# Router logits of fourteen batches computed on GpSimd instead of TensorE, and the choice of experts one batch later, in a fused decoder layer

## The chip, the core and the metric

The kernel runs on one core of a Trainium2 chip. The metric is device time in microseconds for one execution, as the median of several runs. The engines are TensorE (PE; its weight loads are shown as PEld), VectorE (DVE), ScalarE (ACT), GpSimd (POOL) and SyncE (SP, which issues most of the DMAs). Each engine works through its own instructions in a fixed order, and waits for other engines by semaphores.

## The reference

The computation is one decoder layer on x of 16 batches x 256 rows x 256 columns, in float32. It has three stages, each followed by a layer normalization of input plus result:

1. a recurrent block: an input projection to 512 channels, a causal convolution over 4 positions, silu, a projection to 2 x 16 state terms, a scan along the 256 rows, and an output projection;
2. cross attention with 8 heads of 128: queries from x (256 rows), keys and values from 77 context rows and the 256 rows of x (333 in all), softmax, output projection;
3. a mixture of 8 experts. The router is the part that the change touches:

```python
dot = jnp.einsum('bsh,eh->bse', x, expert_embeddings)   # 256 columns -> 8 logits a row
vals, idx = jax.lax.top_k(dot.reshape(n, E), 2)
weights = softmax(where(chosen, dot, -inf))
ones = weights > 0
cap_ones = where(cumsum(ones, axis=0) <= 512, ones, 0)  # each expert takes its first 512 rows
# the chosen rows go through relu(rows @ W1.T) @ W2.T, times the weight, and are added up
```

So for each row of each batch eight dot products of length 256 are needed, then the two largest, then a running count over all rows in order.

## The kernel before

**Tiling.** Rows lie on the 128 partitions; a batch is two tiles of 128 rows. Batches are worked on one after the other, and inside a batch the 8 heads, so the main loop has 128 turns. In turn i TensorE does the key and query products of head i (L512, L517), then the extra steps that are planned for this head, then the output of head i-2 (L564), the scores s of head i (L527), and the transposes pa and pb of head i-1's softmax (L550). VectorE takes the row maximum nm of s (L529), copies the transposed pa to SBUF as ptt (L552), takes the reciprocal rs of the sums (L535) and scales p to pn (L538). ScalarE does exp and most of the copies out of PSUM. GpSimd does small work: the -1/2 powers of the normalizations (r..., L134, called by `rsqrt`), adding the output bias to x (xb, L596), sums of hs for the recurrent block (L305), sums of kvt (tsum, L460 to L463), the output rows o (L624), and the indirect DMAs.

**Extra steps.** A table gives each (batch b, head h) the steps that ride along: `project(b-1)` (the pw products and the second normalization) at heads 2 and 3, `turn_tokens(b-1)` at head 5, `score_experts(b-1)` and `choose(b-1)` at head 6, `dispatch(b-1)` at head 7, `settle(b-1)` (output rows o) at head 7. The steps for the next batch ride there too: in an odd batch `rec_add` and `rec_out` (first normalization of the next two batches) at heads 1 and 3, `prep_norm`, `prep_keys` and `prep_sums` (zl, kvt, tsum), and `prep_values` (pv). The convolutions of the recurrent block (`rec_in`, four chunks for each pair of batches, cv at L297 and L299, hs at L303) ride in batches 0, 1, 2, 4, 5, 6, 8, 9 and 10; in batches 2, 6 and 10 they are at heads 3, 4, 5 and 7, in the others at single heads. The scheduler may move an instruction ahead of that place on its own engine.

**The router before.** `turn_tokens` transposes the normalized rows xs on TensorE (px, four 128x128 products, L649) and VectorE copies them to SBUF (L650). `score_experts` multiplies them by the experts' vectors emb_s (pl, eight products of 8 columns, L658), and VectorE copies the 2 x 8 logits of a row (L666). `choose` finds the two largest with some twenty VectorE instructions of 128x16 or less (L683 to L716). `dispatch` counts with two small products on TensorE (pc, L725, L726), works out the places on VectorE (L728 to L757), and issues four indirect DMAs on GpSimd (L760) that write the rows to their experts. The last two batches (14 and 15) are handled near the end in the same way, at earlier heads.

**Normalization factors.** `again` (L156 to L160, and the power at L134) makes the second factor rlz on GpSimd, which `prep_norm` multiplies into the rows: zl (L425, VectorE), which TensorE then transposes for the keys.

After the main loop the eight experts are worked through (L956 to L1064), some 120 us.

Of the kernel before, what the change touches and what calls it, by code (L numbers as in the profile page):

```python
# [10 lines left out]
F32 = mybir.dt.float32  # L11
I32 = mybir.dt.int32
AF = mybir.ActivationFunctionType
ALU = mybir.AluOpType
AX = mybir.AxisListType
# [3 lines left out]
P = 128  # L19
B, S, D = 16, 256, 256  # L20
# [3 lines left out]
J = S + M  # L24
DI = 512
NST = 16
KC = 4
# [5 lines left out]
GT = S // P  # L33
# [5 lines left out]
def decoder_layer(  # L39
# [20 lines left out]
    bkv,  # L60
    wo,
    bo,
    embT,
    w1T,
    w2T,
# [60 lines left out]
    def apart(group, dma):  # L126
# [2 lines left out]
            tc.declare_no_dep(dma.ins, other.ins, reason="disjoint rows")  # L129
        groups.setdefault(group, []).append(dma)  # L130

    def rsqrt(v, n, rows, name):
        r = small.tile([P, n], F32, tag="r", name=f"r{name}")
        G.tensor_tensor(r[:rows], v[:rows], nhalf[:rows, 0:n], ALU.pow)  # L134
        return r

    def layernorm(dst, src, n, rows, name):
# [42 lines left out]
    gl = wpool.tile([P, DC], F32, tag="gl", name="gl")  # L180
    bl = wpool.tile([P, DC], F32, tag="bl", name="bl")
    emb_s = wpool.tile([P, DC, E], F32, tag="emb", name="emb_s")
    wsum = wpool.tile([P, 4, 512], F32, tag="wsum", name="wsum")

    kvc = wpool.tile([P, DC, B * M], F32, tag="kvc", name="kvc")
# [72 lines left out]
    def load_rest():  # L258
        nc.sync.dma_start(wo_s, wo.rearrange("(h p) f -> p h f", p=P))
        nc.sync.dma_start(bo_s, bo.broadcast_to([P, D]))  # L260
        nc.sync.dma_start(emb_s, embT.rearrange("(c p) e -> p c e", p=P))
    zero = wpool.tile([P, DX], F32, tag="zero", name="zero")
    G.memset(zero, 0.0)
# [18 lines left out]
    def rec_in(pr, c):  # L282

        if c == 0:
            hss[pr] = aw.tile([P, NI, PT], F32, tag="hs", bufs=2, name=f"hs{pr}")
            if pr > 0:
                sums[pr] = aw.tile([P, PT], F32, tag="sums", bufs=2, name=f"sums{pr}")
        ph = bank(f"ph{pr}_{c}")
        for k in range(DC):
            T.matmul(ph, lhsT=inw[:, k, c * P : (c + 1) * P], rhs=xTs[pr][:, k, :], start=(k == 0), stop=(k == DC - 1))  # L290
        hp = a2.tile([P, PB, KC - 1 + S], F32, tag="hp", name=f"hp{pr}_{c}")
        G.memset(hp[:, :, 0 : KC - 1], 0.0)
        A.activation(
            hp[:, :, KC - 1 :], ph.rearrange("p (b s) -> p b s", b=PB), AF.Identity, bias=inb[:, c : c + 1]
        )
        cv = a2.tile([P, PB, S], F32, tag="cv", name=f"cv{pr}_{c}")
        V.tensor_scalar(cv, hp[:, :, 0:S], cw[:, c, 0:1], cb[:, c : c + 1], ALU.mult, ALU.add)  # L297
        for k in range(1, KC):
            V.scalar_tensor_tensor(cv, hp[:, :, k : k + S], cw[:, c, k : k + 1], cv, ALU.mult, ALU.add)  # L299
        z = cv.rearrange("p b s -> p (b s)")  # L300
        th = a2.tile([P, PT], F32, tag="th", name=f"th{pr}_{c}")
        A.activation(th, z, AF.Tanh)
        V.scalar_tensor_tensor(hss[pr][:, c, :], th, 1.0, z, ALU.add, ALU.mult)  # L303
        if c > 0 and pr > 0:
            G.tensor_tensor(sums[pr], hss[pr][:, 0, :] if c == 1 else sums[pr], hss[pr][:, c, :], ALU.add)  # L305

# [110 lines left out]

    stages = {}

    def prep_norm(b):  # L420

        r2 = again(*stats.pop(b), f"z{b}")
        zl = b2.tile([P, 2, D], F32, tag="zl", name=f"zl{b}")
        for i in range(2):
            V.tensor_scalar(zl[:, i, :], xs[b][:, i, 0:D], r2[:, i : i + 1], None, ALU.mult)  # L425
        zs[b] = zl
# [95 lines left out]
    def head_softmax(b, h):  # L522

        kt, qt = kts.pop((b, h)), qts.pop((b, h))
        s = ps.tile([P, 2, 512], F32, tag="s", bufs=1, name=f"s{b}_{h}")
        for ic in range(2):
            T.matmul(s[:, ic, 0:J], lhsT=qt[:, ic * P : (ic + 1) * P], rhs=kt, start=True, stop=True)  # L527
        nm = small.tile([P, 2], F32, tag="nm", name=f"nm{b}_{h}")
        V.tensor_reduce(nm, s[:, :, 0:J], AX.X, ALU.max, negate=True)  # L529
        p = b2.tile([P, 2, J], F32, tag="p", name=f"p{b}_{h}")  # L530
        sm = small.tile([P, 2], F32, tag="sm", name=f"sm{b}_{h}")
        for ic in range(2):
            A.activation(p[:, ic, :], s[:, ic, 0:J], AF.Exp, bias=nm[:, ic : ic + 1], accum_out=sm[:, ic : ic + 1])  # L533
        rs = small.tile([P, 2], F32, tag="rs", name=f"rs{b}_{h}")
        V.reciprocal(rs, sm)  # L535
        pn = b2.tile([P, 2, J], F32, tag="pn", name=f"pn{b}_{h}")
        for ic in range(2):
            V.tensor_scalar(pn[:, ic, :], p[:, ic, :], rs[:, ic : ic + 1], None, ALU.mult)  # L538
        pns[b, h] = pn

    def head_turn(b, h):

# [33 lines left out]
    def project(b, i):  # L576

        ot = outs_t[b]
        if i == 0 or b == B - 1:
            pws[b] = bank(f"pw{b}_{i}")  # L580
        for h in range(H):
            T.matmul(  # L582
                pws[b][:, i * D : (i + 1) * D],
                lhsT=ot[:, h, i * P : (i + 1) * P],
                rhs=wo_s[:, h, :],
                start=(h == 0),
                stop=(h == H - 1),
            )
        if b == B - 1:
            norm_half(b, i)  # L590
            return
        if i == 0:
            return
        xb = b1.tile([P, 2, D], F32, tag="xb", name=f"xb{b}")
        for j in range(2):
            G.tensor_tensor(xb[:, j, :], xs[b][:, j, 0:D], bo_s, ALU.add)  # L596
        y = b2.tile([P, 2, D], F32, tag="yb", name=f"yb{b}")
        V.tensor_tensor(y.rearrange("p i d -> p (i d)"), pws.pop(b), xb.rearrange("p i d -> p (i d)"), ALU.add)  # L598
        norms[b] = layernorm(xs[b], y, 2, P, f"b{b}")

    def norm_half(b, i):

# [16 lines left out]
    def settle(b):  # L619

        r2 = again(*norms.pop(b), f"o{b}")
        o = b2.tile([P, 2, D], F32, tag="yb", name=f"o{b}")
        for j in range(2):
            G.tensor_scalar(o[:, j, :], xs[b][:, j, 0:D], r2[:, j : j + 1], 1.0, ALU.mult, ALU.mult)  # L624
        nc.sync.dma_start(out_f[b * S : (b + 1) * S, :].rearrange("(i p) d -> p i d", p=P), o)
# [26 lines left out]
    def score_experts(b):  # L652

        x2 = x2s.pop(b)
        pl = bank(f"pl{b}")
        for i in range(2):
            for k in range(DC):
                T.matmul(  # L658
                    pl[:, i * E : (i + 1) * E],
                    lhsT=x2[:, k, i * P : (i + 1) * P],  # L660
                    rhs=emb_s[:, k, :],
                    start=(k == 0),
                    stop=(k == DC - 1),
                )
        lgs[b] = small.tile([P, GT, E], F32, tag="lg", bufs=2, name=f"lg{b}")
        V.tensor_copy(lgs[b].rearrange("p t e -> p (t e)"), pl[:, 0 : GT * E])  # L666

    def t3(tag, b):
        return small.tile([P, GT, E], F32, tag=tag, bufs=2, name=f"{tag}_{b}")
# [104 lines left out]
    def at(b, h, f, *args):  # L774
        steps[b, h].append((f, args))

    def behind(b, h, f, *args):

        late_steps[b, h].append((f, args))
# [4 lines left out]
    for b in range(B):  # L784
        nb = b + 1
        new_pair = nb % PB == 0 and nb < B
        if b > 0:
            early = 2 * int(b == B - 1)
            at(b, 2, project, b - 1, 0)
            at(b, 3 - early // 2, project, b - 1, 1)  # L790
            at(b, 5 - early, turn_tokens, b - 1)
            at(b, 6 - early, score_experts, b - 1)
            at(b, 6 - early, choose, b - 1)
            at(b, 7 - early, dispatch, b - 1)
            at(b, 7, settle, b - 1)
        if new_pair:
            if nb == PB:
                at(b, 0, rec_state, nb, nb + 1)
            elif nb % 4 == 0:
                at(b, 0, rec_state, nb, nb + 3)  # L800
            at(b, 1, rec_add, nb)
            at(b, 1, rec_out, nb)
            at(b, 2, prep_norm, nb)
            at(b, 3, rec_out, nb + 1)
            at(b, 3, prep_keys, nb)
            at(b, 3, prep_sums, nb)
            for n, h in enumerate((4, 6, 7)):
                at(b, h, prep_values, nb, n, False)
                behind(b, h, prep_values, nb, n, True)
        elif nb < B:  # L810
            at(b, 0, prep_norm, nb)
            at(b, 0, prep_keys, nb)
            at(b, 0, prep_sums, nb)
            for n, h in enumerate((1, 4, 6)):
                at(b, h, prep_values, nb, n, False)
                behind(b, h, prep_values, nb, n, True)
# [22 lines left out]
    context(3)  # L839
    rec_add(0)  # L840
    rec_out(0)
    prep_norm(0)
    prep_keys(0)
    context(4)
# [231 lines left out]
    for i in range(len(heads) + 2):  # L1076
# [12 lines left out]
            head_softmax(*heads[i])  # L1089
        if 1 <= i <= len(heads):  # L1090
            turned = head_turn(*heads[i - 1])
        if i < len(heads):
            for f, args in late_steps[heads[i]]:
                f(*args)
# [84 lines left out]
```

## Time and profile before

| what | value |
|---|---|
| median of 3 runs | 1200.22 us (1199.39 to 1200.71) |
| the profiled execution's own time | 1201.09 us |
| its span, first to last instruction | 1199.3 us |
| mean granted TensorE clock | 0.991 |
| GpSimd busy | 312.3 us (26%), 560 instructions |
| VectorE busy | 748.6 us (62%) |
| DMA queue of SP | 50.13 MB |

A group line of the profile has the line in the code, the engine, the operation, output <- inputs, partitions x elements and the count; then busy time in us (overlaps counted once), the mean ns of one instruction, and the idle time of the engine just before, with what ended it. A timeline line has the start in us from the span's start, the length in us, the engine, the line and the instruction, "x2" where two in a row are merged, and in brackets idle time before it. A tile line has minimum, median and maximum in ns. A stretch line has, after its bounds and length, the busy time (and the count) of PE, PEld, DVE, ACT and POOL, the granted clock, the DMA share and GB/s.

### The profile page before, as it was taken

What the parts mean: (1) busy time and instruction counts of PE and PEld (TensorE: products, weight loads), DVE (VectorE), ACT (ScalarE), POOL (GpSimd) and SP (SyncE); (2) the same over time, 40 slices, a digit from 0 to 9 for tenths busy, and PEclk for the clock granted to TensorE, in tenths of its full rate; (3) what the DMA queues carried; (4) which work ended last, traced back from release to release, by engine and by line L of the source; (5) the groups of instructions that cost most, each with busy time, mean ns of one, the idle gap of its engine ahead of it and who ended that gap; (6) DMA issues with size and microseconds to landing.
All of it is one profiled execution on the core that took longest, in us unless ns stands there. A gap on an engine that the chain in (4) does not pass through costs nothing. (4 is left out here: it accounts for less than half of the span.)

```text
span 1199.3 us, 15750 instructions
## 1 busy us (share of the span) xinstructions
PE 1152.6 (96%) x5134; PEld 827.8 (69%) x5134; DVE 748.6 (62%) x2226; ACT 485.4 (40%) x1273; POOL 312.3 (26%) x560
## 2 busy tenths in 40 slices
PE   6789999999999999999999999999999999999996
PEld 2337676767777767767777777677777778876664
DVE  5535768596646765874658576756465645666665
ACT  2125434444344434443435343534343433423331
POOL 2200132222221332222213222232122211225554
PEclk8899999999999999999999999999999999999999
DMA  6760001001000110010000000010001000125762
GB/s 207 226 188 11 19 20 37 28 10 56 18 29 9 35 36 23 9 46 18 15 10 23 29 21 9 4 29 4 20 14 45 14 9 3 30 92 171 182 182 85
DMA packets 45402, 60.37 MB, mean 50 GB/s; under 512 B 7813, under 2 KB 35438, under 8 KB 45320
## 3 DMA queue, kind: packets, MB, share of 16 engines
q1 hardware_dynamic: 38552, 50.13, 13.6%
q0 software_dynamic: 6048, 9.22, 3.1%
q8 instruction: 41, 0.67, 0.2%
q14 instruction: 41, 0.34, 0.1%
q10 hardware_dynamic: 720, 0.01, 0.0%
HBM read 36.07 MB, written 30.78 MB: 56 GB/s over the span
## 5 line engine op out<-in xcount | busy, mean ns | idle before, releaser
L564 PE MATMUL po<-ptt,v 128*128 128x256 f32 (+1 forms) x768 | 190.0, 382 | 6.3 <-DVE ptt L552 6.3
L564 PEld LDWEIGHTS po<-ptt,v 128*128 128x128 f32 (+1 forms) x768 | 142.7, 190 | 58.7 <-issue 25.7
L529 DVE TENSOR_REDUCE nm<-s 128x2 f32<-128x666 f32 x128 | 108.3, 846 | 117.1 <-PE s L527 117.1
L512 PE MATMUL pk<-kvt,wkv_s 128*128 128x333 f32 x512 | 164.9, 444 | 0.0
L527 PE MATMUL s<-kt,qt 128*128 128x333 f32 x512 | 164.3, 442 | 0.0
L572 ACT ACTIVATE ot<-po,bkv_s 128x256 f32<-128x256 f32 x128 | 60.8, 475 | 218.9 <-PE po L564 218.7
L533 ACT ACTIVATE p<-s,nm 128x333 f32<-128x333 f32 x256 | 135.4, 535 | 33.7 <-DVE nm L529 32.5
L517 PE MATMUL pq<-kvt,wq_s 128*128 128x256 f32 x512 | 131.2, 378 | 0.0
L512 PEld LDWEIGHTS pk<-kvt,wkv_s 128*128 128x128 f32 x512 | 91.1, 191 | 45.0 <-issue 22.0
L527 PEld LDWEIGHTS s<-kt,qt 128*128 128x128 f32 x512 | 96.4, 188 | 31.3 <-ACT qt L519 0.5
L517 PEld LDWEIGHTS pq<-kvt,wq_s 128*128 128x128 f32 x512 | 96.7, 189 | 30.2
L582 PE MATMUL pw<-wo_s,ot 128*128 128x256 f32 x512 | 115.8, 379 | 0.0
L553 ACT COPY ptt<-pb 77x256 f32<-77x256 f32 x128 | 47.1, 368 | 168.2 <-PE pb L550 168.2
L582 PEld LDWEIGHTS pw<-wo_s,ot 128*128 128x128 f32 x512 | 97.0, 190 | 13.2
L538 DVE TENSOR_SCALAR pn<-p,rs 128x333 f32<-128x333 f32 x256 | 97.8, 416 | 3.8
L760 POOL DMA_INDIRECT xg<-xs,sidx x64 | 66.4, 1038 | 88.7 <-DVE sidx L757 68.0
L550 PEld LDWEIGHTS pa<-ident,pn 128*128 128x128 f32 x512 | 63.6, 141 | 34.8 <-DVE pn L538 6.8
L552 DVE COPY ptt<-pa 128x512 f32<-128x512 f32 x128 | 87.1, 680 | 0.6 <-PE pa L550 0.6
L596 POOL TENSOR_TENSOR xb<-xs,bo_s 128x256 f32<-128x256 f32 x30 | 19.9, 683 | 244.1 <-DVE yb L598 244.1
L550 PE MATMUL pa<-ident,pn 128*128 128x128 f32 x512 | 78.3, 274 | 2.6 <-DVE pn L538 2.6
L514 ACT ACTIVATE kt<-pk,bkv_s 128x333 f32<-128x333 f32 x128 | 69.0, 539 | 19.9 <-PE pk L512 19.6
L299 DVE SCALAR_TENSOR_TENSOR cv<-hp,cw,cv 128x512 f32<-128x512 f32 x96 | 71.8, 751 | 1.9
(231 smaller groups left out, 1670.0 us busy)
## 6 DMA issues: line engine op xcount, KB each, us to landing
v<-vc SPq DMA_DIRECT2D x16, 308.0 KB
vc<-vc SPq DMA_DIRECT2D x9, 512.0 KB
xg<-zero SPq DMA_DIRECT2D x34, 131.0 KB
xe<-xg SPq DMA_DIRECT2D x8, 524.0 KB
xT<-in_xT SPq DMA_DIRECT2D x8, 512.0 KB
xt<-in_x_in SPq DMA_DIRECT2D x16, 256.0 KB
out<-o SPq DMA_DIRECT2D x16, 256.0 KB
w<-in_w1T SPq DMA_DIRECT2D x8, 512.0 KB
```

Source lines behind the costliest of these rows:

```text
L299: V.scalar_tensor_tensor(cv, hp[:, :, k : k + S], cw[:, c, k : k + 1], cv, ALU.mult, ALU.add)
L512: T.matmul(pk[:, 0:J], lhsT=wkv_s[:, k, f], rhs=kvt[:, k, :], start=(k == 0), stop=(k == DC - 1))
L514: A.activation(kt, pk[:, 0:J], AF.Identity, bias=bkv_s[:, h : h + 1])
L517: T.matmul(pq[:, 0:S], lhsT=wq_s[:, k, f], rhs=kvt[:, k, 0:S], start=(k == 0), stop=(k == DC - 1))
L527: T.matmul(s[:, ic, 0:J], lhsT=qt[:, ic * P : (ic + 1) * P], rhs=kt, start=True, stop=True)
L529: V.tensor_reduce(nm, s[:, :, 0:J], AX.X, ALU.max, negate=True)
L533: A.activation(p[:, ic, :], s[:, ic, 0:J], AF.Exp, bias=nm[:, ic : ic + 1], accum_out=sm[:, ic : ic + 1])
L538: V.tensor_scalar(pn[:, ic, :], p[:, ic, :], rs[:, ic : ic + 1], None, ALU.mult)
L550: T.transpose(dst[0:jn, c0 : c0 + P], pn[:, ic, j0 : j0 + jn], ident)
L552: turned = V.tensor_copy(ptt[:, 0:2, :], pt01.rearrange("p (j i) -> p j i", j=2))
L564: T.matmul(po[:, 0:S], lhsT=vs[b][0:jn, jc, h * DH : (h + 1) * DH], rhs=ptt[0:jn, jc, :], start=(jc == 0), stop=(jc == 2),)
L582: T.matmul(pws[b][:, i * D : (i + 1) * D], lhsT=ot[:, h, i * P : (i + 1) * P], rhs=wo_s[:, h, :], start=(h == 0), stop=(h == H - 1),)
```

## The change

For batches 0 to 13 the transposes, the logit products and their copies are gone. In their place `score` runs on GpSimd, in four parts for a batch (two row tiles x two groups of four experts). A part multiplies the row tile, repeated for four experts, by the experts' vectors, which lie on all partitions in the new tile emb_b; then it adds halves onto each other until 32 columns are left. `score_end` lets VectorE add up these 32 columns. The parts are at heads 4 to 7 of batch b for the rows of batch b-1; `score_end` and `choose` come at head 0 of batch b+1, behind the copy ptt, and `dispatch` at head 2 of batch b+1. Batches 14 and 15 keep TensorE's way.

The parts are issued after the factor rlz of a later batch (`factor_ends`), and this factor is now its own step `prep_factors`, ahead of `prep_norm`. SBUF for emb_b (8 KB a partition), the products (4 KB) and the folded parts is made by smaller changes: the tanh is written over the convolution's input hp, the softmax is scaled in place (p with three buffers, no pn), the sum y is written over xb, and zl and o have one buffer instead of two. A DMA of 1 MB brings emb_b to all partitions, after the other weights.

```diff
+    emb_b = wpool.tile([P, E, D], F32, tag="emb_b", name="emb_b")
...
+        nc.sync.dma_start(emb_b.rearrange("p e d -> p (e d)"), emb.broadcast_to([P, E * D]))
...
-        th = a2.tile([P, PT], F32, tag="th", name=f"th{pr}_{c}")
-        A.activation(th, z, AF.Tanh)
+        th = hp[:, :, KC - 1 :]
+        A.activation(th, cv, AF.Tanh)
...
+    def prep_factors(b):
+        factors[b] = again(*stats.pop(b), f"z{b}")
+        factor_ends[b] = powers[-1]
     def prep_norm(b):
-        r2 = again(*stats.pop(b), f"z{b}")
-        zl = b2.tile([P, 2, D], F32, tag="zl", name=f"zl{b}")
+        r2 = factors.pop(b)
+        zl = b1.tile([P, 2, D], F32, tag="zl", name=f"zl{b}")
...
-        p = b2.tile([P, 2, J], F32, tag="p", name=f"p{b}_{h}")
+        p = b2.tile([P, 2, J], F32, tag="p", bufs=3, name=f"p{b}_{h}")
...
-        pn = b2.tile([P, 2, J], F32, tag="pn", name=f"pn{b}_{h}")
         for ic in range(2):
-            V.tensor_scalar(pn[:, ic, :], p[:, ic, :], rs[:, ic : ic + 1], None, ALU.mult)
+            V.tensor_scalar(p[:, ic, :], p[:, ic, :], rs[:, ic : ic + 1], None, ALU.mult)
...
-        y = b2.tile([P, 2, D], F32, tag="yb", name=f"yb{b}")
-        V.tensor_tensor(y.rearrange("p i d -> p (i d)"), pws.pop(b), xb.rearrange("p i d -> p (i d)"), ALU.add)
+        flat = xb.rearrange("p i d -> p (i d)")
+        V.tensor_tensor(flat, pws.pop(b), flat, ALU.add)
...
-        o = b2.tile([P, 2, D], F32, tag="yb", name=f"o{b}")
+        o = b1.tile([P, 2, D], F32, tag="yb", name=f"o{b}")
...
+    EG = 4
+    W = 32
+    def score(b, i, g):
+        after = factor_ends.get(b + 3 if b % 2 == 0 else b + 2)
+        if after is not None:
+            with tc.issue_after(after.ins):
+                score_part(b, i, g)
+        else:
+            score_part(b, i, g)
+    def score_part(b, i, g):
+        if i == 0 and g == 0:
+            parts[b] = b1.tile([P, GT, E, W], F32, tag="x2", name=f"part{b}")
+        x = xs[b][:, i, 0:D].unsqueeze(1).broadcast_to([P, EG, D])
+        e = slice(g * EG, (g + 1) * EG)
+        m = b1.tile([P, EG, D], F32, tag="prod", name=f"prod{b}_{i}_{g}")
+        G.tensor_tensor(m, x, emb_b[:, e, :], ALU.mult)
+        n = D // 2
+        while n > W:
+            G.tensor_tensor(m[:, :, 0:n], m[:, :, 0:n], m[:, :, n : 2 * n], ALU.add)
+            n //= 2
+        G.tensor_tensor(parts[b][:, i, e, :], m[:, :, 0:n], m[:, :, n : 2 * n], ALU.add)
+    def score_end(b):
+        lgs[b] = small.tile([P, GT, E], F32, tag="lg", bufs=2, name=f"lg{b}")
+        V.tensor_reduce(lgs[b], parts.pop(b), AX.X, ALU.add)
...
-            at(b, 5 - early, turn_tokens, b - 1)
-            at(b, 6 - early, score_experts, b - 1)
-            at(b, 6 - early, choose, b - 1)
-            at(b, 7 - early, dispatch, b - 1)
+            if b == B - 1:
+                at(b, 3, turn_tokens, b - 1)
+                at(b, 4, score_experts, b - 1)
+                at(b, 4, choose, b - 1)
+                at(b, 5, dispatch, b - 1)
+            else:
+                for n in range(4):
+                    at(b, 4 + n, score, b - 1, n // 2, n % 2)
+                settled(b + 1, 0, score_end, b - 1)
+                settled(b + 1, 0, choose, b - 1)
+                at(b + 1, 2, dispatch, b - 1)
...
+        if 1 <= i < len(heads):
+            with tc.issue_after(turned.ins):
+                for f, args in turn_steps[heads[i]]:
+                    f(*args)
```

More of the change, by code (lines that the diff above doesn't have):

```diff
@@ L62, in decoder_layer @@
     bo,
+    emb,
     embT,
@@ L130, in apart @@
         groups.setdefault(group, []).append(dma)
+    powers = []
     def rsqrt(v, n, rows, name):
         r = small.tile([P, n], F32, tag="r", name=f"r{name}")
-        G.tensor_tensor(r[:rows], v[:rows], nhalf[:rows, 0:n], ALU.pow)
+        powers.append(G.tensor_tensor(r[:rows], v[:rows], nhalf[:rows, 0:n], ALU.pow))
         return r
@@ L299, in rec_in @@
             V.scalar_tensor_tensor(cv, hp[:, :, k : k + S], cw[:, c, k : k + 1], cv, ALU.mult, ALU.add)
-        z = cv.rearrange("p b s -> p (b s)")
-        th = a2.tile([P, PT], F32, tag="th", name=f"th{pr}_{c}")
-        A.activation(th, z, AF.Tanh)
-        V.scalar_tensor_tensor(hss[pr][:, c, :], th, 1.0, z, ALU.add, ALU.mult)
+        th = hp[:, :, KC - 1 :]
+        A.activation(th, cv, AF.Tanh)
+        V.scalar_tensor_tensor(hss[pr][:, c, :].rearrange("p (b s) -> p b s", b=PB), th, 1.0, cv, ALU.add, ALU.mult)
         if c > 0 and pr > 0:
@@ L418, in decoder_layer @@
     stages = {}
+    factors, factor_ends = {}, {}
+    def prep_factors(b):
+        factors[b] = again(*stats.pop(b), f"z{b}")
+        factor_ends[b] = powers[-1]
     def prep_norm(b):
-        r2 = again(*stats.pop(b), f"z{b}")
-        zl = b2.tile([P, 2, D], F32, tag="zl", name=f"zl{b}")
+        r2 = factors.pop(b)
+        zl = b1.tile([P, 2, D], F32, tag="zl", name=f"zl{b}")
         for i in range(2):
@@ L535, in head_softmax @@
         V.reciprocal(rs, sm)
-        pn = b2.tile([P, 2, J], F32, tag="pn", name=f"pn{b}_{h}")
         for ic in range(2):
-            V.tensor_scalar(pn[:, ic, :], p[:, ic, :], rs[:, ic : ic + 1], None, ALU.mult)
-        pns[b, h] = pn
+            V.tensor_scalar(p[:, ic, :], p[:, ic, :], rs[:, ic : ic + 1], None, ALU.mult)
+        pns[b, h] = p
     def head_turn(b, h):
@@ L596, in project @@
             G.tensor_tensor(xb[:, j, :], xs[b][:, j, 0:D], bo_s, ALU.add)
-        y = b2.tile([P, 2, D], F32, tag="yb", name=f"yb{b}")
-        V.tensor_tensor(y.rearrange("p i d -> p (i d)"), pws.pop(b), xb.rearrange("p i d -> p (i d)"), ALU.add)
-        norms[b] = layernorm(xs[b], y, 2, P, f"b{b}")
+        flat = xb.rearrange("p i d -> p (i d)")
+        V.tensor_tensor(flat, pws.pop(b), flat, ALU.add)
+        norms[b] = layernorm(xs[b], xb, 2, P, f"b{b}")
     def norm_half(b, i):
@@ L666, in score_experts @@
         V.tensor_copy(lgs[b].rearrange("p t e -> p (t e)"), pl[:, 0 : GT * E])
+    EG = 4
+    W = 32
+    parts = {}
+    def score(b, i, g):
[20 more added lines that the diff above has]
+        V.tensor_reduce(lgs[b], parts.pop(b), AX.X, ALU.add)
     def t3(tag, b):
@@ L775, in at, with settled @@
         steps[b, h].append((f, args))
+    turn_steps = {(b, h): [] for b in range(B) for h in range(H)}
+    def settled(b, h, f, *args):
+        turn_steps[b, h].append((f, args))
     def behind(b, h, f, *args):
@@ L802, in decoder_layer @@
             at(b, 1, rec_out, nb)
+            at(b, 2, prep_factors, nb)
             at(b, 2, prep_norm, nb)
             at(b, 3, rec_out, nb + 1)
+            at(b, 3, prep_factors, nb + 1)
             at(b, 3, prep_keys, nb)
@@ L810, in decoder_layer @@
         elif nb < B:
+            if b == 0:
+                at(b, 0, prep_factors, nb)
             at(b, 0, prep_norm, nb)
@@ L841, in decoder_layer @@
     rec_out(0)
+    prep_factors(0)
     prep_norm(0)
@@ L1163 @@
         "bo": a[xa + "bo"].reshape(1, -1),
+        "emb": a[ff + "expert_embeddings"].reshape(1, E * D),
         "embT": a[ff + "expert_embeddings"].T,
```

## The prediction

> **What bounds the kernel now.** I read the page first. The busy rows give TensorE 96%, and the 40 slices show it at 9 from the fourth to the last but one:
>
> ```profile
> PE 1152.6 (96%) x5134; PEld 827.8 (69%) x5134; DVE 748.6 (62%) x2226; ACT 485.4 (40%) x1273; POOL 312.3 (26%) x560
> ```
>
> From 100 to 1,060 us TensorE has hardly a gap, so a matmul that goes is time that goes, unless a new gap opens. The groups by line give the matmuls that go (duration modelled, idle before them 0.0):
>
> ```profile
> L658 PE MATMUL pl<-emb_s,x 128*128 128x8 f32 x120 | 14.3, 245 | 0.0
> L649 PE MATMUL px<-ident,xs 128*128 128x128 f32 x60 | 9.0, 272 | 0.0
> ```
>
> The timeline of a batch shows the one place where TensorE waits regularly: head 3 of an odd batch, here batch 7 (start, length, engine):
>
> ```profile
> 558.11 1.54 PE L564 MATMUL po<-ptt,v 128*128 128x256 f32 x6 [0.85 <-DVE ptt L552]
> 559.48 1.28 PE L527 MATMUL s<-kt,qt 128*128 128x333 f32 x4
> 561.29 0.85 PE L550 MATMUL pa<-ident,pn 128*128 128x128 f32 x4 [0.53 <-DVE pn L538]
> ```
>
> ```profile
> 560.25 0.35 DVE L425 TENSOR_SCALAR zl<-xs,rlz 128x256 f32<-128x256 f32 x1 [2.29 <-POOL rlz L134]
> 560.52 0.16 DVE L535 RECIPROCAL rs<-sm 128x2 f32<-128x2 f32 x1
> 560.60 0.33 DVE L425 TENSOR_SCALAR zl<-xs,rlz 128x256 f32<-128x256 f32 x1
> 560.85 0.69 DVE L538 TENSOR_SCALAR pn<-p,rs 128x333 f32<-128x333 f32 x2
> ```
>
> VectorE sits behind GpSimd's factor rlz, and the transposes pa behind VectorE: no slack there. In most other heads pn is done 2.2 to 4 us before its transposes start (pn of 500.61 ends at 502.31, its pa starts at 504.69).
>
> What VectorE pays when GpSimd streams is in the tile view (min/median/max) and in the timelines of batch 6:
>
> ```profile
> L538 DVE TENSOR_SCALAR pn<-p,rs x256: 379/390/1404, 96.1 to 1051.7; 128x333 f32<-128x333 f32 x128
> ```
>
> ```profile
> 500.61 1.70 DVE L538 TENSOR_SCALAR pn<-p,rs 128x333 f32<-128x333 f32 x2
> ```
>
> ```profile
> 500.78 1.34 POOL L305 TENSOR_TENSOR sums<-hs 128x512 f32<-128x512 f32 x1 [1.83 <-DVE hs L303]
> ```
>
> A pn pair takes 0.69 us. Here it took 1.70: the GpSimd add issued during the first pn, went before the second and held it to its end. The reverse shows in the same batches: conv steps cv (two SBUF inputs) and GpSimd's output rows o hold each other (at 242.5 us one cv took 848 ns instead of 750, one o 892 instead of 482). The row maximum nm keeps 0.85 us with or without GpSimd beside it.
>
> **The change part by part.**
>
> *Removed from TensorE.* Per batch four transposes, 4 x 9.0/60 = 0.60 us, and eight logit products, 8 x 14.3/120 = 0.95. Fourteen batches: 14 x 1.55 = **-21.7 us**. The copies x (0.69) and lg (0.17) leave VectorE; a reduction of 128x512 arrives (about 0.7, from nm's 846 ns for 666 columns). Nothing.
>
> *Added to GpSimd.* Four parts per batch, each a product of 1024 columns and sums of 512, 256 and 128:
>
> ```profile
> L596 POOL TENSOR_TENSOR xb<-xs,bo_s 128x256 f32<-128x256 f32 x30 | 19.9, 683 | 244.1 <-DVE yb L598 244.1
> L305 POOL TENSOR_TENSOR sums<-sums,hs 128x512 f32<-128x512 f32 x14 | 18.2, 1297 | 24.8 <-DVE hs L303 24.8
> ```
>
> From 256 to 512 columns the step is 0.61 us, so 1024 take 1.30 + 2 x 0.61 = 2.53, and 128 take 0.46 (tsum). A part: 2.53 + 1.30 + 0.68 + 0.46 = 4.97 us; a batch 19.9; fourteen 278. GpSimd would be busy 590 us of 1,199: there is room, and the time goes by what its stream holds up.
>
> *Price of a meeting.* The held pair lost 1.01 us to an add of 1.34, so a meeting costs the GpSimd instruction less 0.33: 2.20, 0.97, 0.35 and 0.13, mean 0.91, 14.6 us per batch if every one of the 16 is met.
>
> (a) Head 3 of odd batches. In the new order the first product is the very next GpSimd instruction after rlz, so it meets zl or the reciprocal's successors. pa has no slack: 2.2 us in each of 7 odd batches, **+15.4** (bounds: 0 if zl and pn slip ahead, 7 x 2.53 = 17.7).
>
> (b) Batches 2, 6 and 10 have conv chunks in heads 3, 4 and 5, just where the parts run. VectorE is nearly full there:
>
> ```profile
> 490.80:505.40 14.60, 14.60 (x62) 9.96 (x61) 13.78 (x25) 7.73 (x19) 1.97 (x4) 1.00 0.05 18
> ```
>
> (TensorE 14.60, VectorE 13.78, GpSimd 1.97 of 14.60 us.) Each of these heads has 7 instructions that can meet: one cv scaling, three cv steps, hs, two pn; 21 against 16 parts' instructions and 4 of o and xb (together 1.0 us). What runs beside nm, ptt, rs and the v addition (0.85 + 0.68 + 0.17 + 0.68 = 2.4 of 6.4 us, 37%) costs nothing: (14.6 + 1.0) x 0.63 = 9.8, less 2.4 of slack: 7.4 us a batch, **+22** (bounds: 0, and 3 x 15.6 = 47).
>
> (c) Single chunks fall among the parts in head 5 of batches 1, 4, 5, 8 and 9: 7 x 0.91 x 0.63 = 4.0, less 2.4: 1.6 each, **+8** (0 to 32).
>
> (d) Other heads: two pn, 1.8 us, below the slack of some 2.8: 0 (the worst pair, product then 512 add, 3.2).
>
> The row comes first, but the Trainium skill speaks to the same thing: "SBUF — State Buffer", section "Who interferes with whom", says that GpSimd and VectorE share a port pair, that an instruction in a 2-port mode takes it for its whole length and the other side blocks, that two SBUF inputs on VectorE contend with GpSimd's reads, and that a reduction never does. The held pn and the unchanged nm agree. Taken literally a meeting costs the whole instruction, not 0.33 less; the sum below would then be about +46 instead of +24, an estimate from that page. It speaks against the change.
>
> *Moved.* Choice goes from head 6 to head 0 of the next batch: about 21 small VectorE instructions of 0.17 us, 3.5 us. In an odd head 0 VectorE has 1.9 us idle of 7.2, so with the reduction nm of head 1 comes 2.3 late; behind it wait exp and pn of head 1, whose slack is 4.1: 0, and up to 7 x 2.3 = 16 if that cover were gone. If GpSimd is late, the reduction stands at the front of VectorE with rs, pn and the next nm behind it. Dispatch moves to head 2: its four DMA issues (about 1.3 us apart, 5.1 us) now stand in GpSimd's queue before rb, the factor of the second normalization, which is ready only at 552.8 in batch 7 when they would run from 543.7 to 548.8: 0 (late by all of it: 14 x 5). Its two small products are moved ahead of pw on TensorE, their input is a head old: 0.
>
> *The rest.* The tanh written over hp, the softmax scaled in place with three buffers, y in xb, single zl and o: each buffer's last reader is at least a head older than the next writer (zl: read at 549.9, written at 560.3): 0. The broadcast load of 1 MB enters SP's queue after the weights, ahead of vc, xT and v; six clears move behind them: 0, at most 5.5 us at the 190 GB/s of the page's first slices.
>
> **Sum** for the profiled execution (1,201.09 us; span 1,199.3): -21.7 + 15.4 + 22 + 8 = +23.7, so 1,224.8. The median lies 0.9 lower: **1,224 us, slower**.
>
> **Rivals.**
> - *The holds are absorbed* (faster). VectorE has 38% idle, loses the copy x, and head 6 loses its choice; if zl and pn slip ahead in (a) and (b), (c) stay within the slack, the time is 1,200 - 21.7 = 1,179, with half of (a) 1,186. It decides at 21.7 us of stalls: 1.55 per batch. For it: TensorE's slack of 2 to 4 us almost everywhere. Against: (a) has none, and 13.78 of 14.60.
> - *GpSimd late.* In plain odd batches parts start at 560.2 and need 19.9, plus o, xb and 16 waits of up to 0.4: to 587 or later; tsum (1.9 us) stands behind and pv needs it at 590.9. If strided or broadcast operands make a part 2.5 us longer, 10 us a batch, 5 to 6 of it stall TensorE in some 6 batches: +33, about 1,257.
> - *A draw.* (a) in full and half of (c) and nothing else: within 2.4 us of before.
>
> **Chances.** Holds cost more than the matmuls (forecast, 1,203 to 1,250): 0.55. GpSimd late as well: 0.12. Absorbed: 0.28. Draw: 0.05. So slower by over 0.2% (about what a measurement of this kernel can tell from no change) 0.67, within 0.05, faster 0.28. The bounds of (a) to (c) reach from 1,179 to 1,275; leaving out the lowest of the faster case and the top of the late one gives 1,184 to 1,258; the forecast's own range is 1,203 to 1,250.
>
> **What would show it.** pn's and cv's maxima: pn to about 2.6 us, cv to 3, dozens of instances; nm unchanged at 0.85. TensorE's idle time before pa in odd head 3 from 0.5 to 2.7 us; gaps before pa in heads 3 to 5 of batches 2, 6 and 10; GpSimd near 590 us with products of 2.5 us. px and pl down to two batches. Wrong if pn waits but pa does not, if the products come in pieces that let VectorE through, or if GpSimd's instructions give way.

## The result, and the profile after

The changed kernel takes 1235.37 us (median of four runs, 1232.99 to 1236.41) against 1199.81 us before: ratio 1.0294, 95% interval 1.0275 to 1.0313. It is slower by some 35 us, inside the predicted range and on the predicted side, 11 us above the predicted time. Its profiled execution has a span of 1231.2 us (before: 1199.3) and a mean granted clock of 0.983 (before: 0.991).

The busy rows of the page after:

```profile
PE 1148.1 (93%) x4966; PEld 816.9 (66%) x4966; DVE 844.6 (69%) x2212; ACT 485.3 (39%) x1273; POOL 587.7 (48%) x784
```

The 168 matmuls are gone (14 x 12), yet TensorE is busy only 4.5 us less, and VectorE is busy 96 us more with 14 instructions fewer. GpSimd's 588 us are what was forecast. The groups of the page show its products (busy, mean ns of one) and the row maximum:

```profile
L699 POOL TENSOR_TENSOR prod<-xs,emb_b 128x1024 f32<-128x1024 f32 x56 | 124.0, 2215 | 2.7
...
L541 DVE TENSOR_REDUCE nm<-s 128x2 f32<-128x666 f32 x128 | 108.2, 845 | 104.2 <-PE s L539 104.2
```

The products take 2.2 us (forecast 2.5), and nm does not notice them (846 ns before, 845 after). VectorE instructions that work from SBUF to SBUF do. The tile views (minimum/median/maximum ns) of p, cv and zl:

```profile
L549 DVE TENSOR_SCALAR p<-p,rs x256: 373/395/2461, 93.4 to 1084.5; 128x333 f32<-128x333 f32 x128
```

```profile
L304 DVE SCALAR_TENSOR_TENSOR cv<-hp,cw,cv x96: 734/752/2725, 13.9 to 803.1; 128x512 f32<-128x512 f32 x96
```

```profile
L437 DVE TENSOR_SCALAR zl<-xs,rlz x32: 324/350/2433, 48.6 to 956.2; 128x256 f32<-128x256 f32 x32
```

The medians are as before and the maxima are the median plus one GpSimd product. The 48 cv steps with no GpSimd arithmetic beside them average 746 ns, the 48 with some 1,418.

**Head 3 of batch 7**, the place of step (a). Timelines of VectorE, GpSimd and TensorE (start, length):

```profile
580.90 2.43 DVE L437 TENSOR_SCALAR zl<-xs,rlz 128x256 f32<-128x256 f32 x1 [1.13 <-POOL rlz L137]
583.26 0.15 DVE L547 RECIPROCAL rs<-sm 128x2 f32<-128x2 f32 x1
583.33 0.33 DVE L437 TENSOR_SCALAR zl<-xs,rlz 128x256 f32<-128x256 f32 x1
583.58 0.68 DVE L549 TENSOR_SCALAR p<-p,rs 128x333 f32<-128x333 f32 x2
```

```profile
580.17 0.70 POOL L137 TENSOR_TENSOR rlz<-u3z,nhalf 128x2 f32<-128x2 f32 x1
580.84 2.34 POOL L699 TENSOR_TENSOR prod<-xs,emb_b 128x1024 f32<-128x1024 f32 x1
```

```profile
584.02 0.85 PE L561 MATMUL pa<-ident,p 128*128 128x128 f32 x4 [1.44 <-DVE p L549]
```

The product starts 0.06 us before zl, zl lasts until it ends (2.43 us instead of 0.35), p and the transposes pa follow late.

**Batch 6**, the place of step (b), VectorE, GpSimd and TensorE:

```profile
517.97 2.25 DVE L304 SCALAR_TENSOR_TENSOR cv<-hp,cw,cv 128x512 f32<-128x512 f32 x1
520.14 0.68 DVE L563 COPY ptt<-pa 128x512 f32<-128x512 f32 x1
```

```profile
517.67 2.00 POOL L699 TENSOR_TENSOR prod<-xs,emb_b 128x1024 f32<-128x1024 f32 x1
```

```profile
520.96 2.90 PE L575 MATMUL po<-ptt,v 128*128 128x256 f32 x6 [3.82 <-ACT hp L307]
```

A cv step is held behind a product; ptt, which is not held itself (680 ns in the mean before and after), stands behind it in VectorE's queue and ends at 520.82; po, which reads ptt, starts 0.14 us later, after 3.8 us of idle time. The profile names ScalarE's hp as the releaser, the tanh of the same held cv, because it ended last (520.94); po reads ptt, not hp. The list of TensorE's waits (total us, times, longest) has this pair 13 times, where the list of before has none:

```profile
PE po L575 <- ACT hp L307: 25.7, 13, 3.8
PE pa L561 <- DVE p L549: 9.6, 8, 1.4
```

po now takes 2.90 us for 6 matmuls instead of 1.53: the windows behind that gap show the granted clock (third figure from the end):

```profile
505.00:519.00 14.00, 11.11 (x40) 6.44 (x38) 13.89 (x14) 4.92 (x13) 13.59 (x13) 1.00 0.06 20
519.00:521.00 2.00, 0.04 (x1) 0.07 (x1) 2.00 (x4) 0.92 (x4) 1.92 (x2) 0.90 0.00 0
521.00:526.00 5.00, 5.00 (x11) 3.48 (x12) 4.96 (x6) 1.78 (x4) 4.73 (x6) 0.50 0.00 0
```

VectorE is full (13.89 of 14.00), GpSimd too, TensorE waits; and then it runs at half clock until 527.4.

**Head 0 of batches 5 and 9.** One more wait of the same list is new, and no GpSimd part runs beside it:

```profile
PE po L575 <- DVE oh L732: 3.7, 2, 1.9
```

In batches 5 and 9 the moved choice shares head 0 with a convolution chunk and the first normalization. Its small instructions stand between them in VectorE's queue, ptt comes late behind all of them (at 421.2 us in batch 5), and po waits 1.85 us in each of the two batches.

### The profile page after: what moved, and what is told of

The parts are those of the page before. It is cut to its first block, busy times and chain, and to the rows that moved or that the text cites. A ratio compares the mean times of both kernels' runs of the same rounds, so it can differ in the third digit from the quotient of the medians.

```text
span 1231.2 us, 15427 instructions
## 1 busy us (share of the span) xinstructions
PE 1148.1 (93%) x4966; PEld 816.9 (66%) x4966; DVE 844.6 (69%) x2212; ACT 485.3 (39%) x1273; POOL 587.7 (48%) x784
## 5 line engine op out<-in xcount | busy, mean ns | idle before, releaser
L575 PE MATMUL po<-ptt,v 128*128 128x256 f32 (+1 forms) x768 | 197.0, 392 | 39.1 <-ACT hp L307 25.7
L575 PEld LDWEIGHTS po<-ptt,v 128*128 128x128 f32 (+1 forms) x768 | 145.2, 194 | 98.2 <-ACT hp L307 36.1
L539 PE MATMUL s<-kt,qt 128*128 128x333 f32 x512 | 169.6, 453 | 0.0
L549 DVE TENSOR_SCALAR p<-p,rs 128x333 f32<-128x333 f32 x256 | 136.1, 567 | 3.3
L699 POOL TENSOR_TENSOR prod<-xs,emb_b 128x1024 f32<-128x1024 f32 x56 | 124.0, 2215 | 2.7
L702 POOL TENSOR_TENSOR prod<-prod 128x512 f32<-128x512 f32 x112 | 119.9, 1070 | 6.8
L539 PEld LDWEIGHTS s<-kt,qt 128*128 128x128 f32 x512 | 99.4, 194 | 32.8 <-issue 2.4
L304 DVE SCALAR_TENSOR_TENSOR cv<-hp,cw,cv 128x512 f32<-128x512 f32 x96 | 103.7, 1083 | 1.9
L561 PEld LDWEIGHTS pa<-ident,p 128*128 128x128 f32 x512 | 64.6, 143 | 43.6 <-DVE p L549 15.1
L561 PE MATMUL pa<-ident,p 128*128 128x128 f32 x512 | 80.1, 278 | 9.6 <-DVE p L549 9.6
```

Source lines behind the costliest of these rows:

```text
L549: V.tensor_scalar(p[:, ic, :], p[:, ic, :], rs[:, ic : ic + 1], None, ALU.mult)
L561: T.transpose(dst[0:jn, c0 : c0 + P], pn[:, ic, j0 : j0 + jn], ident)
L575: T.matmul(po[:, 0:S], lhsT=vs[b][0:jn, jc, h * DH : (h + 1) * DH], rhs=ptt[0:jn, jc, :], start=(jc == 0), stop=(jc == 2),)
L699: G.tensor_tensor(m, x, emb_b[:, e, :], ALU.mult)
L702: G.tensor_tensor(m[:, :, 0:n], m[:, :, 0:n], m[:, :, n : 2 * n], ALU.add)
```

## The experiments

Ratios are to runs of the kernel before on the same chip. The theory: GpSimd's arithmetic holds VectorE's SBUF instructions, and time is lost where one of these has no slack (zl in odd head 3) or many lie in a full queue (conv chunks). The rivals: GpSimd is late; the other edits (choice, buffers, load) cost it; VectorE is too full wherever the work lies.

**1. Logits on TensorE, all other edits kept.**

```diff
-                for n in range(4):
-                    at(b, 4 + n, score, b - 1, n // 2, n % 2)
-                settled(b + 1, 0, score_end, b - 1)
+                at(b, 5, turn_tokens, b - 1)
+                at(b, 6, score_experts, b - 1)
```

> The changed kernel with the logits back on TensorE (px at head 5, pl at head 6), everything else as changed: late choice and dispatch, merged buffers, load of emb_b. Theory (GpSimd's stream holds VectorE through the shared port): nothing streams, so about the time of before, 1,198 to 1,203. Rival 1 (the later choice and dispatch, or the merged buffers, cost the time): 1,210 or more, with the gaps of head 1 in batches 5 and 9 still there. Both agree that it is below 1,235.

Measured: 1200.03 us, 1.0008 (0.9998 to 1.0017). The other edits cost nothing in sum, but single ones gain and lose: where the choice meets a chunk in head 0 (batches 5 and 9), 1.3 and 3.1 us are lost. TensorE has a gap of 2.06 us in both batches; in batch 9 alone 3.4 us at half clock follow it. In odd head 3, rlz comes sooner and TensorE's idle time falls from 1.4 to 0.9 us.

**2. No parts, no logits on TensorE.** `score` is not called; the logits are 32-column sums of xs.

> The changed kernel without GpSimd's parts: the logits are sums over 32 columns of the rows themselves, one VectorE reduction for each row tile, so the routing is another one. It shows what the removed TensorE work is worth with nothing in its place. Theory: 21.7 us below before, 1,176 to 1,181. Rival 1 (choice and buffers cost something): above 1,185. Rival 2 (a removed matmul is not worth its duration, because another engine sets the pace): above 1,190.

Measured: 1176.97 us, 0.9817 (0.9801 to 0.9834). From run 1 to run 2 the time falls by 23.1 us (forecast for the removed TensorE work: 21.7). Batch by batch, from one batch's first nm to the next one's, it is 1.33 us in twelve of the fourteen batches, but 2.6 and 4.3 in batches 5 and 9, where run 1 waits longer for the choice. So the removed work itself is worth 14 x 1.33 = 18.6 us, and 4.3 are that wait. From here to the changed kernel it is 58.4 us, almost all of it the price of the parts.

**3. Fills instead of parts.** As 2, with fills of emb_b in each part's place:

```diff
+        m = emb_b.rearrange("p e d -> p (e d)")
+        for n in (2048, 1400, 1000, 700, 500):
+            G.memset(m[:, 0:n], 1.0)
```

> As e2_no_parts, but GpSimd is kept as long at the same places of its queue by five fills a part (2048, 1400, 1000, 700, 500 columns, about 5 us by the page's fill of 262 columns in 0.31 us), which write and read nothing. Theory (reads of GpSimd hold VectorE's second input): cv and hs keep 0.75 and 0.69 us, only the scalings p, zl and the cv scaling are held; 1,178 to 1,195. Rival 1 (GpSimd's queue being late sets the time, whatever it does): 1,225 to 1,240. Rival 3 (any GpSimd instruction holds VectorE, reading or not): cv's mean as long as in the changed kernel, 1,225 to 1,240, told from rival 1 by cv's durations.

Measured: 1229.76 us, 1.0252 (1.0235 to 1.0269). The cv steps are free again (at most 902 ns), but the time is not, which looks like a refutation. TensorE's waits show that it is lost elsewhere:

```profile
PE pv L489 <- DVE oh L725: 10.1, 3, 3.4
PE pv L489 <- DVE oh2m L749: 9.1, 2, 4.5
PE pv L489 <- POOL tsum L474: 8.8, 1, 8.8
```

These waits lie in head 0 of even batches (1.6 to 8.8 us of TensorE's idle time in each of them); batches 2, 6 and 10 have no gap in heads 3 to 5. The fills take longer than the parts (GpSimd is busy 606.9 us) and wait for no row, so they stand elsewhere in GpSimd's queue, and tsum and the choice come late behind them. That is the second rival, GpSimd late, made by the experiment and not by the change: this run could not decide. Run 7 mends it.

**4. Short parts**, `EG = 1`: sixteen parts a batch of 256, 128, 64 and 32 columns.

> The changed kernel with one expert in a part instead of four: 16 parts a batch, each of 256, 128, 64 and 32 columns. GpSimd works longer (by its rows some 27 us a batch instead of 20), each instruction is short. Theory (a meeting costs VectorE the rest of one GpSimd instruction): the longest hold falls from 2.5 to 0.6 us, batches 2, 6 and 10 lose most of their gaps, 1,185 to 1,210. Rival 1 (GpSimd's lateness): later than now, 1,245 or more. Rival 4 (it is GpSimd's total share of the port that counts, not the length of a piece): 1,235 to 1,250.

Measured: 1316.83 us, 1.0986 (1.0967 to 1.1004); a miss. Held cv steps shrink (maximum 1,631 ns), but the short instructions cost more per column (four products of 256 columns take 4 x 0.71 us, one of 1024 columns 2.2): GpSimd is busy 717.7 us, no longer fits between the rows and the next batch's sums, and head 0 of even batches loses 7 to 12 us each against run 2. Heads 4 and 6 of batches 2, 6 and 10 lose another 4.5 and 7.1 to 7.9: a chunk's first cv step waits there (5.2 and 8.3 us in batch 6) for a fill of hp that stands late in GpSimd's queue. So the late GpSimd is a real danger; the changed kernel, with its 20 us a batch, stays short of it.

**5. Conv chunks out of the way** in batches 2, 6 and 10.

```diff
-        for c, h in enumerate((3, 4, 5, 7)):
+        for c, h in enumerate((1, 2, 6, 7)):
```

> As the changed kernel, but the convolution chunks of batches 2, 6 and 10 are planned at heads 1, 2, 6 and 7 instead of 3, 4, 5 and 7, so none of them lies beside the GpSimd parts (which run from the second normalization in head 3 to head 5). Theory (what is lost in these batches is conv steps held by GpSimd, with ptt and so po queued behind them): against the run with the logits on TensorE these three batches lost 8.3, 8.3 and 10.0 us; without the meeting they should cost about what batches 12 and 14 do, -1.3 each, so the time goes from 1235.4 to about 1205 (1200 to 1212), the half-clock pieces at 260, 519 and 780 us are gone and the clock is near 0.989. Rival 1 (VectorE simply has too much work in these batches, wherever the chunks lie, or the parts hold p and zl as badly): 1225 or more. Rival 2 (the clock pieces come from something else than the gaps): about 1222, with the pieces still there.

Measured: 1211.61 us, 1.0111 (1.0089 to 1.0133): 23.8 us come back (1235.4 less 1211.6), at the upper edge of the theory's range (one of the four runs took 1215.94). The three batches now take 67.0 us each instead of 74.7, 74.6 and 76.3, and their half-clock stretches are gone. The waits of po for hp fall from 13 to 4 (those in other batches), while pa's stay:

```profile
PE pa L561 <- DVE p L549: 9.3, 8, 1.3
...
PE po L575 <- ACT hp L307: 6.3, 4, 1.9
```

**6. The first product behind p** in odd batches.

```diff
+        if i == 0 and g == 0 and b % 2 == 0:
+            G.tensor_copy(m[:, 0, 0:1], pns[b + 1, 3][:, 1, 0:1])
         G.tensor_tensor(m, x, emb_b[:, e, :], ALU.mult)
```

> As the changed kernel, but in odd batches the first GpSimd product has to wait for the softmax scaling p of head 3 (a copy of one column of p into the product's tile stands ahead of it), so it can no longer meet zl and p of that head. Theory (step a of the prediction: zl is held 2.1 us by this product, and the transposes pa have no slack): 2.0 us in each of seven odd batches come back, 1235.4 - 14 = 1221 (1218 to 1225), zl at most 0.35 us long in odd head 3, pa's idle there under 0.5 us. Rival (the hold passes on to the next scaling or to ptt, or the later parts make the next batch's sums late): 1232 to 1238.

Measured: 1230.10 us, 1.0246 (1.0229 to 1.0263): 5 us came back instead of 14, between theory and rival. The tile view shows that zl is held no more by a product:

```profile
L437 DVE TENSOR_SCALAR zl<-xs,rlz x32: 326/350/800, 51.4 to 953.3; 128x256 f32<-128x256 f32 x32
```

Batches 3, 7, 11 and 13 gave back 1.7, 1.9, 1.7 and 2.7 us, as the theory has it. Batch 1 gave back 3.7, but there 6.8 us at half clock went as well, so this is not step (a) alone. In batches 5 and 9 the later parts run further into the chunk of head 5: each has a gap of 3.8 us there instead of 1.9, with 3.4 us at half clock behind it, and loses 1.8 and 1.9 us more in all. Batches 2 and 6 lost 1.7 more and batch 10 1.7 less, at places that the edit does not touch; the half-clock stretches there, and the gaps behind them, come out differently. So the hold did pass on in two batches, though to a chunk and not, as the rival had it, to p or ptt.

**7. Fills on time.** As 3, but three fills (2048, 1400, 700), each part behind a copy of one column of xs. GpSimd is busy 535.2 us, less than the 587.7 of the changed kernel, so the durations beside the fills decide here, and the time only supports them.

> Leaves the router's real logits out: the logits are the sums of 32 columns of xs. Each of the four parts is replaced by one copy of a column of xs (so that it starts when the part would) and three fills of 2048, 1400 and 700 columns, some 3.8 us a part against 4.9, so GpSimd is done before the next batch needs it; GpSimd writes but hardly reads. Theory (conv steps with two inputs are held by GpSimd's reads, the one-input scalings zl and p and the first conv step by any long GpSimd instruction): no cv step above 0.95 us apart from the first, p and zl up to 1.8; the time is 1177.0 (no parts at all) plus up to 1.5 us in seven odd batches plus up to 3 in batches 2, 6 and 10: 1184 to 1197. Rival 1 (every GpSimd instruction holds VectorE, whatever it does): cv up to 2.6 us, 1215 or more. Rival 2 (what costs time is not the holding but the order of GpSimd's queue): 1215 or more with cv short.

Measured: 1191.16 us, 0.9926 (0.9909 to 0.9942), inside the theory's range. The tile views:

```profile
L304 DVE SCALAR_TENSOR_TENSOR cv<-hp,cw,cv x96: 735/751/1422, 14.7 to 761.9; 128x512 f32<-128x512 f32 x96
```

```profile
L549 DVE TENSOR_SCALAR p<-p,rs x256: 373/396/2024, 95.9 to 1041.5; 128x333 f32<-128x333 f32 x128
```

The 30 cv steps that have only the parts' fills beside them take 748 ns in the mean and 753 at most; the three above 1,400 stood beside sums. (The forecast of no cv above 0.95 forgot these.) Scalings p beside fills alone average 1,069 ns. So here a GpSimd instruction that only writes does not hold a cv step, which has two SBUF inputs, and one that reads does; the scaling p with one input is held by both.

**8. Put together.** The edits of 5 and 6, with batches 0, 4 and 8 back on TensorE.

> The whole computation, put together from the findings: chunks of batches 2, 6 and 10 moved as in the run before, the first product of odd batches behind p, and the logits of batches 0, 4 and 8 (whose parts would meet chunks in batches 1, 5 and 9) back on TensorE. Theory: against the run with all logits on TensorE (1200.0) eleven batches save 1.55 us each, 17 us; batches 4 and 8 still meet chunks in heads 5 and 7, 1.9 us each, and other heads lose some 0.3: 1200 - 17 + 4 + 3 = 1190 (1184 to 1195), faster than the kernel before. Rival (the parts hold whatever else is there, and each saved microsecond is lost again): 1198 to 1210.

Measured: 1192.89 us, 0.9945 (0.9929 to 0.9962), inside the theory's range. Batches 5 and 9 now have no parts beside them, and the wait for the choice is still there, so it belongs to the choice and the chunk:

```profile
PE po L575 <- DVE oh L734: 3.6, 2, 1.8
```

**9. The single chunks moved too.** As 8, with only batch 0 back on TensorE, and the single chunks moved as well:

```diff
-        first = ((1, 1), (1, 3), (1, 5), (1, 7)) if nb == 4 else ((0, 5), (0, 7), (1, 0), (1, 5))
+        first = ((1, 1), (1, 3), (1, 5), (1, 7)) if nb == 4 else ((0, 1), (0, 2), (0, 7), (1, 1))
```

> The whole computation. As the run that put the findings together, but the single chunks go out of the parts' way too: those of batches 4 and 5 (and 8 and 9) from heads 5, 7, 0 and 5 to heads 1, 2 and 7 of the even batch and head 1 of the odd one, so chunk and choice no longer meet in head 0 either; and the logits of batches 4 and 8 are back on GpSimd (only batch 0's stay on TensorE, besides the last two). Theory (a part costs nothing where no chunk lies beside it): batches 5 and 9 go from +1.2 to -2.2 as batches 3, 7 and 11 did, batches 4 and 8 from +0.1 to -0.5: 1192.9 - 6.8 - 1.2 = 1185 (1182 to 1189). Rival (the even batch's VectorE is too full with three chunks at heads 1, 2 and 7, or the parts find the choice and the second normalization instead): 1192 or more.

Measured: 1183.14 us, 0.9855 (0.9830 to 0.9880): the same GpSimd parts in thirteen batches, 52 us below the changed kernel and 16 below the kernel before. Its busy rows and its groups of po and pa:

```profile
PE 1135.7 (96%) x4978; PEld 811.1 (69%) x4978; DVE 802.9 (68%) x2213; ACT 484.6 (41%) x1273; POOL 556.4 (47%) x774
...
L575 PE MATMUL po<-ptt,v 128*128 128x256 f32 (+1 forms) x768 | 190.4, 382 | 6.8 <-DVE ptt L563 6.8
...
L561 PE MATMUL pa<-ident,p 128*128 128x128 f32 x512 | 78.3, 273 | 0.3
```

Idle time before po is 6.8 us (before: 6.3, after: 39.1), before pa 0.3 (after: 9.6). GpSimd still holds p: in the tile view its maximum is 2,133 ns. In batches 3, 7, 11, 12 and 13, which take within 0.01 us of their time in run 2, this costs nothing: these p have slack. The wait for the choice in batches 5 and 9 is gone too, since no chunk lies in head 0 any more. Not everything is clear: one cv step in each of batches 2, 6 and 10 still meets a product (2.37 us), and these batches take 1.9 to 2.0 us more than in run 2.

**10. Control:** logits on TensorE, chunks of batches 2, 6 and 10 moved as in 5.

> Control: all logits on TensorE as in the first run, with the chunks of batches 2, 6 and 10 moved to heads 1, 2, 6 and 7 as in the run with moved chunks. Theory (moving the chunks is worth nothing by itself, what they gain there is the meeting): 1200 (1198 to 1203), so that the parts alone cost 1211.6 - 1200 = 11 us more than TensorE's logits when the chunks are out of their way, the 14 of step a and some 11 of the chunks in the other batches less the 21.7. Rival (the move itself frees or costs TensorE some us): below 1197 or above 1204.

Measured: 1200.60 us, 1.0010 (0.9997 to 1.0022). Moving the chunks of batches 2, 6 and 10 is worth nothing by itself; what run 5 gained is the meeting.

## Why the prediction was right, step by step

The parts' own price can be read batch by batch, as the time from one batch's first nm to the next one's, changed kernel less run 2: batches 1 to 14 lose 7.4, 9.7, 1.7, 1.6, 5.1, 9.6, 1.8, 1.6, 5.0, 11.3, 1.7, 0.0, 2.7 and 0.0 us, 59.2 in all.

| step | forecast | measured |
|---|---|---|
| removed from TensorE | -21.7 | -18.6 (run 1 to run 2, 1.33 in each of 14 batches) |
| moved choice, buffers, load | 0 | -5.5 (before to run 2, batch by batch, less the row above) |
| (a) odd head 3: 1.7, 1.8, 1.7 in batches 3, 7, 11, 2.7 in 13; 1.7 taken for 1, 5 and 9 | +15.4 | +13.1 |
| (b) batches 2, 6, 10 | +22 | +30.7 |
| (c) rest of batches 1, 5, 9 and batches 4, 8 | +8 | +15.4 |
| (d) other heads (batches 12, 14) | 0 | 0.0 |
| sum | +23.7 | +35.1 (medians: +35.6) |

The direction and the mechanism were right: GpSimd's products hold VectorE's SBUF instructions, and TensorE waits where these have no slack. That the number stayed in the range also took some luck. Two costs stand at nothing in the sum, the half clock (some 13.6 us) and the wait for the choice, while the first three rows of the table together came out 4.7 us lower than forecast.

*Removed work:* a saving on the bounding engine, as forecast, but 1.33 us a batch and not 1.55.

*Moved:* put at 0. The order of the new steps brings rlz sooner, which run 1 shows by itself (batches 3, 7 and 11 are 0.9 us shorter there than before). Against this stands the wait for the choice in batches 5 and 9, where the choice meets a chunk in head 0: 1.85 us each in the changed kernel, of which run 2 has 0.76 as well; the rest stands in row (c). The prediction had looked at head 0 of odd batches, but not at those with a chunk in it.

*Step (a):* right in place and mechanism, 2.2 forecast and 1.7 measured for a batch; head 3 alone grew by 2.0 to 2.1 us against run 2 in batches 3, 5, 7, 9 and 11. Set against the kernel before, odd head 3 grew by only 0.6 us, since rlz comes sooner, and the idle time before pa in batch 7 rose from 0.53 to 1.44 us where the prediction expected 2.7.

*Steps (b) and (c):* the mechanism was right, the size too small and the place of the gap wrong. The prediction put the gaps "before pa", on the argument that p is what TensorE waits for. They open before po: a held cv stands ahead of ptt in VectorE's queue, and p is late only behind it. And the terms took a stall as idle time only. Each gap of 2.4 to 3.8 us in batches 1, 2, 6 and 10 was followed by half clock, 6.8 us in each batch. TensorE's busy time in each of these four is 3.5 to 4.1 us above that of run 2 with the same matmuls; in the other batches it is 0.7 at most. Half of 4 x 6.8 us, 13.6, is the estimate for the clock: 10.2 in (b) and 3.4 in (c). Without it (b) would be 20.5, near the forecast 22 although the gaps were elsewhere, and (c) 12.0 instead of 8. Of these 12.0, batches 4 and 8 have 3.1 (forecast 3.2), and the longer wait for the choice is 2.2.

*The price of a meeting,* "GpSimd's instruction less 0.33": the zl above lost 2.08 us to a product of 2.34, started 0.06 before it, so 0.26 less; close.

The Trainium skill ("SBUF — State Buffer", "Who interferes with whom") was weighed against that price. Runs 3 and 7 agree with its distinction of reads and writes for two-input VectorE instructions (753 ns at most beside fills, against 1,418 in the mean beside arithmetic). The prediction's estimate by the literal rule, the whole instruction, made the sum +46 instead of +24, so (a) to (c) together about 68 us instead of 45.4. Measured are 59.2, and without the estimated 13.6 of half clock 45.6; so most of what the forecast lacked lay in the clock and not in the 0.33.

*The rivals.* "The holds are absorbed" fell: 58.4 us lie between run 2 and the changed kernel. Yet run 9 reaches 1,183, the middle of what that rival had named (1,179 to 1,186), once little without slack lies beside the parts. "VectorE is too full wherever the work lies" fell with runs 5 and 9. "GpSimd late" did not occur in the changed kernel; runs 3 and 4 show what it looks like, and that its point is near: 607 us of GpSimd work instead of 588, in a worse order, were enough for it.

What stays open: of batch 1's 7.4 us some 3.4 are the half clock; how the rest splits between (a) and the chunk was not tried, and 1.7 for (a) there is taken from the other odd batches.

## What to carry to other kernels

When work goes to GpSimd, list what VectorE does beside each instruction, and which of it has slack on the way to the bounding engine: here the price was a little less than one GpSimd instruction per meeting (2.08 us beside a product of 2.34), and TensorE paid it only where a queue had no slack. Look at everything that stands behind the held instruction in VectorE's queue, not only at the instruction itself. If the parts can't move, move what they meet: here moving the convolution chunks of three batches was worth 24 us and one wait for p some 2 us in an odd batch without chunks, and with the rest moved as well the loss turned into a gain.

## What was not expected of the hardware

The granted clock of TensorE falls to 0.50 behind single gaps. In the main loop of before TensorE has no gap of 1.5 us or more, and the clock stays at 1.00. In the changed kernel gaps of 2.9 us (at 194 us) and 3.8 us (at 258.5 and 517.1) were each followed by about 6.8 us at 0.50, gaps of 3.8 us (at 775.8) and 2.4 us (at 787.4) by about 3.4 us each; four gaps of 1.85 to 1.95 us were followed by none. At half speed for so long, the same gap of 3.8 us cost, beyond its own length, an estimated 3.4 us at one place and half of that at another. The length of a gap alone does not tell what follows: in run 1 one gap of 2.06 us was followed by 3.4 us at 0.50 and the other by none, in run 5 one of two gaps of 1.86 us was, and in run 3 two gaps of 3.4 us were followed by 6.8 us and a third by none. The Trainium skill ("TensorE: Matmul & The Clock Gate", "HAM oscillation — how this bites in real kernels") warns of idle gaps longer than some 3.4 us; here gaps of 2.4 and 2.9 us did it as well, and sometimes one of 1.9 or 2.1.
